# A four-layer modulated convolution on one core: stage 1 of the weight chain by six products, one sum of the inputs by an accumulating DMA, three sums an iteration sooner

## The chip, the cores and the metric

One core of a Trainium2 chip runs the whole kernel. The metric is the device time of one launch in microseconds (us). Each kernel was run several times; the median is quoted with the lowest and the highest run.

The engines carry the profile's names: PE multiplies matrices (PEld is the loading of its weights, which overlaps), DVE and POOL do elementwise work, ACT does scaled copies, SP starts most DMAs. Each takes its instructions in order and waits on semaphores for the others.

## The reference

128 sequences `x` of 64 channels and 1024 positions go through four convolutions of three taps. The weights of each are scaled per sequence and input channel by a style vector and normalised per sequence and output channel; the second doubles the length, the last halves it, both with a blur by (1, 3, 3, 1) / 8. The result is added to `x`. Cut to what matters:

```python
TYPES = ('same', 'upsample', 'same', 'downsample')

def _layer(x, style, w, b, mw, mb, typ):
    s = style @ mw.T + mb
    weight = SCALE * w * s[:, None, :, None]
    demod = lax.rsqrt(jnp.sum(weight * weight, axis=(2, 3)) + EPS)
    weight = weight * demod[:, :, None, None]
    if typ == 'same':
        out = jax.vmap(_conv_same)(x, weight) + b[None, :, None]
    elif typ == 'upsample':
        out = jax.vmap(_conv_up)(x, weight.transpose(0, 2, 1, 3)) + b[None, :, None]
        out = _blur(out, 2.0 * blur_k, (1, 1))
    elif typ == 'downsample':
        xb = _blur(x, blur_k, (2, 2))
        out = jax.vmap(_conv_down)(xb, weight) + b[None, :, None]
    return out

out = x
for i, typ in enumerate(TYPES):
    out = _layer(out, style, weights[i], biases[i], mod_w[i], mod_b[i], typ)
return x + out
```

Everything is float32. No layer has a nonlinearity, so for each sequence the four layers and the sum with `x` are one convolution of nine taps (apart from the ends, which are computed by themselves). The kernel uses that.

## The kernel before

**Units and tiles.** The 128 sequences are 32 units of four (`NQ` = 32). Two sequences share the 128 partitions (64 channels each) and two more lie side by side, so that a group of four matmuls of 64 by 64 serves the four sequences at once. A unit's input tile `X` holds three planes: the positions by their remainder modulo 3.

**The weight chain.** For each unit the four layers' weights are multiplied into nine taps. `scale3` (ACT) makes `wd`, the last layer's three taps with their scales, and beside them sums of taps (`w3x`). *Stage 1* multiplies them by the third layer's taps to the five taps `S`. Each product of one tap by one tap is a block of 64 columns. The first three units and unit 6 go through `stage1`, the plain nine blocks; the other 28 go through `stage1_a` and `stage1_b`, which share products: with a0, a1, a2 and b0, b1, b2 the taps, a0b1 + a1b0 is (a0+a1)(b0+b1) - a0b0 - a1b1. Between the halves ACT copies `psS` with a scale into `S`; after the second half DVE subtracts (line 481) and POOL adds (line 484). *Stage 2* (`stage2`, with `share`) brings in the second layer and the blur and gives `R`; ACT copies it out, POOL forms two sums of taps (`r_sums`, line 638). *Stage 3* (`stage3_b`, `stage3_a`) brings in the first layer and gives `Wf`, from which DVE combines the taps `H` (`combine_a`, `combine_b`).

**The convolution.** It goes by five products of three groups each instead of nine taps. The inputs are sums of the planes: `G` holds planes half of one minus another (`in_g01`, `in_g2`, both DVE, line 712); T1 and T2 are sum and difference of two planes of `G` (`in1`, line 776, and `in2`, line 781, both POOL, one tile `T12`); T0 and T4 lie in `T04` (`in04`, DVE, line 790); T3 is a difference of planes of `X` (`in3`, DVE, line 761). `conv0` to `conv4` are the products, all through line 803; conv4 gathers in `Y`, the others in `psA`. `sum1` and `sum2` (DVE) put partial results together, `output` (ACT) writes them with scale and bias, `store` sends them off.

**The order.** It is written out by hand. `turn_of(q)` is one turn of the main loop and works on several units at once: the end of the convolution of unit q (conv2, conv4, conv0, outputs), the beginning for n = q + 1 (conv3, conv1), stages 2 and 3 and the input sums for c = q + 2, and stage 1 for s = q + 4. Units 0 to 3 go through `early_turn`, the last three through code of their own. `T12` and `T04` have two buffers, `G` has one, `psS`, `psR` and `psW` share one pair of PSUM banks. `SIDE`, `LATE` and `TABLES` hang small jobs of DVE and POOL, mostly for the ends of the sequences, into certain turns.

**What one turn does, in order.** PE: stage 2 of c, conv2 of q, `stage3_b` of c, conv4 of q, `stage3_a` of c, conv3 of n, `stage1_a` of s, conv0 of q, `stage1_b` of s, `share` for c + 1, conv1 of n. DVE: sum2, the combining of taps, T0/T4 of n, the sums for `share` (line 501), the two parts of `G` of c with a side job and stage 1's subtraction between them, sum1, T3 of c. POOL: `r_sums`, T2 of n, the addition in `S`, T1 of c.

Of the kernel before, what the change touches and what calls it, by code (L numbers as in the profile page):

```python
# [54 lines left out]
C = 64  # L55
K = 3
# [7 lines left out]
def kernel(  # L64
# [30 lines left out]
    gpool = ctx.enter_context(tc.tile_pool(name="gpool", bufs=1))  # L95
# [308 lines left out]
    w3x = const.tile([P, 5, C], F32, name="w3x")  # L404
    w2n = const.tile([P, 5, C], F32, name="w2n")
# [9 lines left out]
    def scale3(q, engs=(nc_a, nc_a)):  # L415
# [3 lines left out]
        for j in range(2):  # L419
            t = wd_pool.tile([P, 5, C], F32, tag="wd", name=f"wd{q}_{j}")  # L420
# [23 lines left out]
    EVEN = slice(0, K, 2)  # L444

    def stage1(q, pool=None, engs=(nc_a, nc_a), between=None):
# [9 lines left out]
        for r in range(2):  # L456
            scaled_copy(engs[r], flat(st[r][:, 1:6]), ps[r][:, : 5 * C], tB[:, q, r : r + 1])
# [3 lines left out]
    def stage1_a(q, ps=None):  # L461
# [3 lines left out]
        tap_matmul(ps, wd, 2, 2, w2n[:, 0, :], EVEN, first=True)  # L465
        tap_matmul(ps, wd, 3, 2, w2n[:, 2, :], EVEN)
        tap_matmul(ps, wd, 1, 1, w2n[:, 1, :], slice(1, 2))
        st, t = s_tiles(q)
        for r in range(2):
            scaled_copy(nc_a, flat(st[r][:, :4]), ps[r][:, C : 5 * C], tBn[:, q, r : r + 1])  # L470
        chain[q] = wd, ps, st, t

    def stage1_b(q):

        wd, ps, st, t = chain[q]
        tap_matmul(ps, wd, 2, 1, w2n[:, 3, :], slice(3, 4))
        tap_matmul(ps, wd, 4, 1, w2n[:, 4, :], slice(4, 5), last=True)
        for r in range(2):
            p1 = st[r][:, 0:1, :].to_broadcast([P, 2, C])
            sums = ps[r][:, 2 * C : 6 * C].rearrange("c (a b o) -> c a b o", a=2, b=2)[:, :, 0]  # L480
            nc_v.scalar_tensor_tensor(
                st[r][:, 4:6, :], sums, tB[:, q, r : r + 1], p1, op0=ALU.mult, op1=ALU.subtract
            )
        nc_g.tensor_add(t[:, :, 2], t[:, :, 2], t[:, :, 0])  # L484
# [14 lines left out]
    def share_sums(q):  # L499
        t = whole[q]  # L500
        nc_v.tensor_add(t[:, :, 6:8], t[:, :, 1:5:3], t[:, :, 2:6:3])
# [13 lines left out]
    def share(q, ps):  # L515
# [3 lines left out]
        chain_matmul(p12, E[:, 2], chain[q], slice(6, 7))  # L519
        chain_matmul(p34, E[:, 6], chain[q], slice(6, 7))  # L520
        chain_matmul(p34, E[:, 5], chain[q], slice(7, 8), True)
# [1200 lines left out]
```

## Time and profile before

| | |
|---|---|
| median of 3 runs | 475.84 us (475.61 to 476.85) |
| span of the profiled execution | 475.5 us |
| DVE busy | 417.3 us (88%) |
| ACT busy | 312.0 us (66%) |
| POOL busy | 165.8 us (35%) |
| queue of SP's DMAs, share of 16 DMA engines | 46.3% |
| matmul records of line 803, 64x340 | 3840 |

The profiled execution is one of its own. Its span lies 0.34 us below the median of the runs; a difference worked out against the span is carried over to the median as it is. Times in the timeline count from the start of the span. A row of the timeline merges equal instructions that follow each other; its second number is the time from the start of the first to the end of the last. In a matmul's row that end lies behind the start of the next row, since a matmul's results come out after the next one has entered; how long PE is taken is therefore read from the start of one row to the start of the next.

### The profile page before, as it was taken

The page shows a single profiled execution, that of the slowest core. Times are in us where ns is not written, and L with a number is a line of the kernel's source. Part 1 is how long each engine was busy: PE and PEld are TensorE (multiplying, and loading weights), DVE is VectorE, ACT ScalarE, POOL GpSimd, SP SyncE. Part 2 cuts the span into 40 slices and gives each one's busy share as a digit, 9 for nine tenths or more (in the row PEclk, how much of TensorE's full clock was granted, in tenths as well). Part 3 has the DMA queues.
Part 4 walks back from the last instruction along what each step waited for, and adds up shares of the span by engine and source line. Part 5 has one row for each costly group of instructions (what it writes and reads, how often), then busy time and mean ns, then how long its engine had stood idle before and what let it go on. Part 6 is the DMA issues. An engine that isn't in the chain of part 4 may idle for free.

```text
span 475.5 us, 26771 instructions
## 1 busy us (share of the span) xinstructions
PE 469.7 (99%) x11932; PEld 349.5 (74%) x11932; DVE 417.3 (88%) x694; ACT 312.0 (66%) x711; POOL 165.8 (35%) x200
## 2 busy tenths in 40 slices
PE   9999999999999999999999999999999999999996
PEld 6987788777678876677776677766788787876653
DVE  3889998879989998899979899979998999999896
ACT  4565657577766676766667666667666777766464
POOL 3634033664444342233432233422333423243200
PEclk9999999999999999999999999999999999999999
DMA  5237456535445554345544454543555544455225
GB/s 176 71 115 224 150 151 180 152 113 177 139 145 166 166 166 136 123 150 169 163 150 126 130 168 152 178 124 121 152 164 169 164 145 147 148 152 161 80 91 193
DMA packets 52707, 70.71 MB, mean 149 GB/s; under 512 B 6000, under 2 KB 50672, under 8 KB 52592
## 3 DMA queue, kind: packets, MB, share of 16 engines
q1 hardware_dynamic: 52368, 68.78, 46.3%
q8 instruction: 93, 1.52, 1.4%
q10 hardware_dynamic: 224, 0.22, 0.1%
q14 instruction: 22, 0.18, 0.1%
HBM read 35.36 MB, written 33.62 MB: 145 GB/s over the span
## 4 chain that ended last, share of the span: by engine, by line
PE 99%; DVE 0%; ACT 0%; issue 0%
PE psA L803 47%; PE Y L803 12%; PE psR L506 9%; PE psW L621 7%; PE psA L621 7%; PE psS L428 6%; PE psR L589 5%; PE psA L506 2%; PE Y L1044 2%; PE Y L183 1%; PE Y L379 1%; PE psM L220 0%; PE psE L1044 0%; PE Y L255 0%; DVE o L882 0%; PE psM L255 0%
## 5 line engine op out<-in xcount | busy, mean ns | idle before, releaser
L803 PE MATMUL psA<-T,H 64*64 64x340 f32 x2304 | 185.9, 446 | 0.0
L803 PEld LDWEIGHTS psA<-T,H 64*64 64x64 f32 x2304 | 90.7, 133 | 46.9 <-issue 2.5
L712 DVE SCALAR_TENSOR_TENSOR G<-X 128x1376 f32<-128x1376 f32 (+2 forms) x65 | 78.0, 1206 | 0.2
L776 POOL TENSOR_TENSOR T<-G 128x684 f32<-128x684 f32 x28 | 46.3, 1652 | 73.7 <-DVE G L712 73.7
L484 POOL TENSOR_TENSOR S<-S 128x128 f32<-128x128 f32 x28 | 21.6, 772 | 139.7 <-ACT S L399 139.6
L399 ACT ACTIVATE R<-psR,tC 128x448 f32<-128x448 f32 x63 | 36.6, 631 | 43.6 <-PE psR L506 25.8
L803 PE MATMUL psA<-T,Wf 64*64 64x340 f32 x768 | 63.7, 446 | 0.0
L803 PE MATMUL Y<-T,Wf 64*64 64x340 f32 x768 | 62.4, 451 | 0.0
L712 DVE SCALAR_TENSOR_TENSOR Y<-m,psA 128x340 f32<-128x340 f32 x62 | 32.0, 516 | 28.2 <-PE psA L803 26.9
L399 ACT ACTIVATE psW<-psA 128x128 f32<-128x128 f32 x100 | 19.3, 268 | 49.1 <-PE psA L621 45.0
L790 DVE TENSOR_TENSOR T<-G 128x1368 f32<-128x1368 f32 (+1 forms) x33 | 50.8, 1541 | 0.0
L399 ACT ACTIVATE Wf<-psW,t 128x256 f32<-128x256 f32 (+2 forms) x76 | 32.7, 480 | 26.7 <-PE psW L621 26.4
L761 DVE TENSOR_TENSOR T<-X 128x684 f32<-128x684 f32 x32 | 47.7, 1492 | 0.0
L506 PE MATMUL psR<-S,E 64*64 64x64 f32 (+1 forms) x1472 | 46.8, 237 | 0.0
L781 POOL TENSOR_TENSOR T<-G 128x684 f32<-128x684 f32 x28 | 46.5, 1660 | 0.0
L428 PEld LDWEIGHTS psS<-wd,w2n 64*64 64x64 f32 x1120 | 35.1, 133 | 12.9 <-issue 0.3
L506 PEld LDWEIGHTS psR<-S,E 64*64 64x64 f32 x1472 | 39.5, 134 | 4.9 <-ACT psR L529 0.2
L803 PEld LDWEIGHTS Y<-T,Wf 64*64 64x64 f32 x768 | 30.3, 132 | 16.8
L803 PEld LDWEIGHTS psA<-T,Wf 64*64 64x64 f32 x768 | 29.8, 133 | 14.5
L880 ACT ACTIVATE o<-psA,tb,td 128x340 f32<-128x340 f32 x63 | 37.1, 648 | 5.0 <-PE psA L803 2.8
L880 ACT ACTIVATE o<-y,tb,td 128x340 f32<-128x340 f32 x62 | 38.5, 678 | 0.0
L880 ACT ACTIVATE o<-Y,tb,td 128x340 f32<-128x340 f32 x62 | 36.1, 639 | 2.8 <-PE Y L803 2.0
(180 smaller groups left out, 840.4 us busy)
## 6 DMA issues: line engine op xcount, KB each, us to landing
out<-o SPq DMA_DIRECT2D x191, 170.0 KB, 2.6
X<-in_x SPq DMA_DIRECT2D x150, 172.0 KB, 3.4
X<-in_x SPq DMA_DIRECT2D x14, 516.0 KB, 5.0
par<-in_params SPq DMA_DIRECT2D x3, 192.0 KB, 3.8
Xe<-in_x_ends SPq DMA_DIRECT2D x1, 512.0 KB, 4.5
out<-Oe SPq DMA_DIRECT2D x2, 96.0 KB, 2.1
out<-o ACTq DMA_DIRECT2D x1, 170.0 KB, 2.8
par<-in_params SPq DMA_DIRECT2D x1, 160.0 KB, 2.7
```

Source lines behind the costliest of these rows:

```text
L399: nc_a.activation(dst, src, AF.Copy, scale=f)
L428: nc.tensor.matmul(ps[r][cols, at * C : (at + n) * C], weight[rows], wd[c if r == 0 else 1 - c][rows, taps], start=first, stop=last, skip_ ...
L506: nc.tensor.matmul(dst[r][cols], weight[rows], st[c if r == 0 else 1 - c][rows, slots, :], start=False, stop=last, skip_group_check=True,)
L589: nc.tensor.matmul(ps[r][cols, lo * C : (lo + m) * C], E[rows, e + 2, :], src[rows, a, :], start=(n == 0), stop=(n == 8), skip_group_check ...
L621: nc.tensor.matmul(dst[r][cols], weight[rows], t[rows, c, slots, :], start=first, stop=last, skip_group_check=True,)
L712: nc_v.scalar_tensor_tensor(out, x, f, y, op0=ALU.mult, op1=op)
L761: nc_v.tensor_sub(t[:, pairs, 0, :NJ], plane(X, 3, pairs), plane(X, 1, pairs))
L776: eng.tensor_add(t[:, :, 0, :NJ], plane(g, 2), plane(g, 1))
L781: eng.tensor_sub(t[:, :, 1, :NJ], plane(g, 2), plane(g, 1))
L790: nc_v.tensor_sub(t[:, pairs, :, :NJ], both(a, PL), both(b, 1))
L803: nc.tensor.matmul(ps[s][cols, :NB], w, Ts[q, tag][rows, c, i, g : g + NB], start=(g == 0 and (m == 3 or alone)), stop=(g == K - 1), skip_ ...
L880: nc_a.activation(dst, src, AF.Identity, bias=add, scale=d3)
```

## The change

It has three parts.

**Stage 1 by six products.** `w3x` and `w2n` get a sixth block, the sum of taps 0 and 2. `stage1_a` now makes the products a0b0, a2b2, a1b1 in one block each, `stage1_b` the three products of sums. That leaves out one block of 64 columns in each of the 28 units. ACT copies the first three products by four copies of 128 columns in place of two of 256; POOL forms a0b0 + a2b2 - a1b1 by two instructions (lines 472 and 473) in place of one, and DVE's subtraction, now 192 columns wide in place of 128, reads POOL's result. The plain `stage1` takes its nine blocks as three of 192 columns. The slots of `S` are numbered anew, and what reads them follows.

**T1 by DMA.** `in1` on POOL is replaced from the sixth turn (q = 5) on by `in1_dma`: a DMA that POOL issues right behind `r_sums` and that adds one plane of `G` onto the other in place. conv1 reads T1 out of `G`. `G` gets two buffers for that; to make room, the tile `raw` moves into `Ye` and `g1` into `nw`.

**Other sums sooner.** T0/T4 of a unit are formed at the end of the turn before (behind T3), T2 on POOL likewise ahead of it, and both parts of `G` stand together, ahead of the side job and of stage 1's subtraction.

```diff
-    gpool = ctx.enter_context(tc.tile_pool(name="gpool", bufs=1))
+    gpool = ctx.enter_context(tc.tile_pool(name="gpool", bufs=2))
...
         for t, src in ((w3x, w3), (w2n, woi[2])):
-            nc_g.tensor_add(t[:, K:], src[:, : K - 1], src[:, 1:])
+            nc_g.tensor_add(t[:, K : K + 2], src[:, : K - 1], src[:, 1:])
+            nc_g.tensor_add(t[:, K + 2], src[:, 0], src[:, 2])
...
-        for k, (at, at1) in enumerate(((0, 3), (3, 1), (1, 4))):
-            tap_matmul(ps, wd, at, 2, woi[2][:, k, :], EVEN, first=k == 0)
-            tap_matmul(ps, wd, at1, 1, woi[2][:, k, :], slice(1, 2), last=k == K - 1)
+        for k in range(K):
+            tap_matmul(ps, wd, k, K, woi[2][:, k, :], slice(0, K), first=k == 0, last=k == K - 1)
...
     def stage1_a(q, ps=None):
-        tap_matmul(ps, wd, 2, 2, w2n[:, 0, :], EVEN, first=True)
-        tap_matmul(ps, wd, 3, 2, w2n[:, 2, :], EVEN)
-        tap_matmul(ps, wd, 1, 1, w2n[:, 1, :], slice(1, 2))
+        for n, (i, at) in enumerate(((0, 1), (2, 3), (1, 4))):
+            tap_matmul(ps, wd, at, 1, w2n[:, i, :], slice(i, i + 1), first=n == 0)
         st, t = s_tiles(q)
         for r in range(2):
-            scaled_copy(nc_a, flat(st[r][:, :4]), ps[r][:, C : 5 * C], tBn[:, q, r : r + 1])
+            ends = ps[r][:, C : 5 * C].rearrange("c (a b o) -> c a b o", a=2, b=2)[:, :, 0]
+            scaled_copy(nc_a, st[r][:, 0:5:4, :], ends, tBn[:, q, r : r + 1])
+        for r in range(2):
+            middle = ps[r][:, None, 4 * C : 5 * C].to_broadcast([P, 2, C])
+            scaled_copy(nc_a, st[r][:, 5:8:2, :], middle, tBn[:, q, r : r + 1])
+        nc_g.tensor_add(t[:, :, 6], t[:, :, 0], t[:, :, 4])
+        nc_g.tensor_sub(t[:, :, 6], t[:, :, 6], t[:, :, 5])
...
     def stage1_b(q):
-        tap_matmul(ps, wd, 2, 1, w2n[:, 3, :], slice(3, 4))
-        tap_matmul(ps, wd, 4, 1, w2n[:, 4, :], slice(4, 5), last=True)
+        for n, (i, at) in enumerate(((3, 1), (4, 3), (5, 2))):
+            tap_matmul(ps, wd, at, 1, w2n[:, i, :], slice(i, i + 1), last=n == K - 1)
         for r in range(2):
-            p1 = st[r][:, 0:1, :].to_broadcast([P, 2, C])
-            sums = ps[r][:, 2 * C : 6 * C].rearrange("c (a b o) -> c a b o", a=2, b=2)[:, :, 0]
             nc_v.scalar_tensor_tensor(
-                st[r][:, 4:6, :], sums, tB[:, q, r : r + 1], p1, op0=ALU.mult, op1=ALU.subtract
+                flat(st[r][:, 1:4]),
+                ps[r][:, C : 4 * C],
+                tB[:, q, r : r + 1],
+                flat(st[r][:, 5:8]),
+                op0=ALU.mult,
+                op1=ALU.subtract,
             )
-        nc_g.tensor_add(t[:, :, 2], t[:, :, 2], t[:, :, 0])
...
+    def in1_dma(q):
+        g = Gs[q]
+        nc_g.dma_start(plane(g, 2), plane(g, 1), accum_op=ALU.add)
+        first_of[q] = g[:, :, :PL]
...
     def turn_of(q):
             conv2(q)
             r_sums(c, nc_g)
+            in1_dma(n)
             sum2(q)
-            in2(n, nc_g)
...
-        in04(n)
+        if entry:
+            in04(n)
         if sharing(q):
             share_sums(c + 1)
         in_g2(c)
+        in_g01(c)
         side(SIDE, q)
...
             stage1_b(s)
-        in_g01(c)
...
+        in2(c, nc_g)
         sum1(n)
         in3(c)
         side(LATE, q)
-        if s == NQ:
-            in04(c)
-        in1(c, nc_g)
+        in04(c)
```

The rows below are those of one turn, q = 12 (so n = 13, c = 14, s = 16), first before and then after the change.

PE, stage 1 of unit 16, first half: each row is one matmul, `psS_0` and `psS_1` are the two banks, `wd_0` and `wd_1` the two tiles of scaled taps. Before, the first half:

```order
L428 MATMUL psS_0_3977<-wd_0_3798,w2n 64x128
L428 MATMUL psS_0_3977<-wd_1_3800,w2n 64x128
L428 MATMUL psS_1_3978<-wd_1_3800,w2n 64x128
L428 MATMUL psS_1_3978<-wd_0_3798,w2n 64x128
```

Twice these four and then four of 64x64 make up the first half before, 8 of 64x64 the second half: 20 matmuls. After:

```order
L429 MATMUL psS_0_4015<-wd_0_3836,w2n 64x64
L429 MATMUL psS_0_4015<-wd_1_3838,w2n 64x64
L429 MATMUL psS_1_4016<-wd_1_3838,w2n 64x64
L429 MATMUL psS_1_4016<-wd_0_3836,w2n 64x64
```

Three times these four now stand in each half, 24 matmuls, all of 64 columns.

DVE from the end of the combining of taps to sum2's first step (`Y<-`) in the next turn. Before:

```order
L790 TENSOR_TENSOR T_13_3996<-G_3729 128x4x342
L501 TENSOR_TENSOR S_3721<-S_3721 128x2x128
L712 SCALAR_TENSOR_TENSOR G_3999<-X_105 128x2x342
L1066 TENSOR_TENSOR Ye_161<-Ye_161,c_156 128x64x6
L481 SCALAR_TENSOR_TENSOR S_3991<-psS_0_3977,tB,S_3991 128x128
L481 SCALAR_TENSOR_TENSOR S_3991<-psS_1_3978,tB,S_3991 128x128
L712 SCALAR_TENSOR_TENSOR G_3999<-X_105 128x2x688
L712 SCALAR_TENSOR_TENSOR y_13_4062<-psA_3884,m_13_3994 128x680
L761 TENSOR_TENSOR T_14_4064<-X_105 128x2x342
L712 SCALAR_TENSOR_TENSOR Y<-m_13_3994,psA_3884 128x340 x2
```

After:

```order
L506 TENSOR_TENSOR S_3752<-S_3752 128x2x128
L717 SCALAR_TENSOR_TENSOR G_4039<-X_105 128x2x342
L717 SCALAR_TENSOR_TENSOR G_4039<-X_105 128x2x688
L1082 TENSOR_TENSOR Ye_159<-Ye_159,c_155 128x64x6
L482 SCALAR_TENSOR_TENSOR S_4029<-psS_0_4015,tB,S_4029 128x192
L482 SCALAR_TENSOR_TENSOR S_4029<-psS_1_4016,tB,S_4029 128x192
L717 SCALAR_TENSOR_TENSOR y_13_4107<-psA_3922,m_13_4036 128x680
L766 TENSOR_TENSOR T_14_4109<-X_105 128x2x342
L803 TENSOR_TENSOR T_14_4111<-G_4039 128x4x342
L717 SCALAR_TENSOR_TENSOR Y<-m_13_4036,psA_3922 128x340 x2
```

T0/T4 went from the head of this stretch (for unit 13) to its tail (for unit 14), right ahead of `Y<-`; the large part of `G` went ahead of the side job (`Ye`) and of stage 1's subtraction.

POOL over the same turn. Before:

```order
L638 TENSOR_TENSOR R_3858<-R_3858 128x2x128
L781 TENSOR_TENSOR T_13_3796<-G_3729 128x2x342
L484 TENSOR_TENSOR S_3991<-S_3991 128x2x64
L776 TENSOR_TENSOR T_14_4066<-G_3999 128x2x342
```

After:

```order
L643 TENSOR_TENSOR R_3896<-R_3896 128x2x128
L786 DMA G_3762<-G_3762 128x2x342
L472 TENSOR_TENSOR S_4029<-S_4029 128x2x64
L473 TENSOR_TENSOR S_4029<-S_4029 128x2x64
L794 TENSOR_TENSOR T_14_4105<-G_4039 128x2x342
```

The DMA for unit 13 stands behind `R`'s sums, where T2 of unit 13 was; T1's place at the turn's end is taken by T2 of unit 14, and stage 1 has two POOL instructions, which are ahead of the subtraction on DVE now.

More of the change, by code (lines that the diff above doesn't have):

```diff
@@ L401, in scaled_copy @@
             eng.tensor_scalar(dst, src, f, None, op0=ALU.mult)
-    w3x = const.tile([P, 5, C], F32, name="w3x")
-    w2n = const.tile([P, 5, C], F32, name="w2n")
+    w3x = const.tile([P, 6, C], F32, name="w3x")
+    w2n = const.tile([P, 6, C], F32, name="w2n")
     def split_weights():
@@ L518, in share @@
         p12, p34 = ([b[:, i:j] for b in ps] for i, j in zip(at, at[1:]))
[L519 to L521 removed]
+        chain_matmul(p12, E[:, 2], chain[q], slice(5, 6))
+        chain_matmul(p34, E[:, 6], chain[q], slice(5, 6))
+        chain_matmul(p34, E[:, 5], chain[q], slice(6, 7), True)
         shared_ps[q] = [b[:, at[0] : at[2]] for b in ps]
@@ L795, in product @@
         tag, i = SLOT[m]
+        if m == 1 and q in first_of:
+            src = first_of[q]
+        else:
+            src = Ts[q, tag][:, :, i]
         for g in groups:
@@ L805, in product @@
                         w,
-                        Ts[q, tag][rows, c, i, g : g + NB],
+                        src[rows, c, g : g + NB],
                         start=(g == 0 and (m == 3 or alone)),
@@ L1560 @@
     q, n, c = NQ - 3, NQ - 2, NQ - 1
+    in1_dma(n)
     stage2(c)
     conv2(q)
-    in2(n, nc_g)
     stage3(c, 0)
```

40 lines of the change are left out of this document (20 added, 20 removed).

## The prediction

> **What bounds the kernel now.** I read the page's first lines, then the waits of PE, then one turn of the main loop in the timeline.
>
> ```profile
> span 475.5 us, 26771 instructions
> ## 1 busy us (share of the span) xinstructions
> PE 469.7 (99%) x11932; PEld 349.5 (74%) x11932; DVE 417.3 (88%) x694; ACT 312.0 (66%) x711; POOL 165.8 (35%) x200
> ```
>
> ```profile
> PE Y L183 <- DVE eps L155: 1.0, 1, 1.0
> PE psA L621 <- issue: 0.2, 1, 0.2
> ```
>
> The two rows of the second fence are all that PE ever waited for: 1.2 us in 475.5. But a PE row counts as busy while results drain, so 99% does not show that matmuls enter without pause. That takes the starts of neighbouring rows. Turn q = 12:
>
> ```profile
> 210.53 0.73 PE L428 MATMUL psS<-wd,w2n 64*64 64x128 f32 x24
> 211.08 1.90 PE L803 MATMUL psA<-T,Wf 64*64 64x340 f32 x24
> 212.80 0.41 PE L428 MATMUL psS<-wd,w2n 64*64 64x64 f32 x16
> 213.03 0.53 PE L506 MATMUL psA<-S,E 64*64 64x64 f32 x24
> 213.38 1.90 PE L803 MATMUL psA<-T,H 64*64 64x340 f32 x24
> 215.10 0.40 PE L506 MATMUL psR<-S,E 64*64 64x128 f32 x8
> ```
>
> 24 matmuls of 340 columns take 1.72 us from start to start at both places where the rows show it (211.08 to 212.80, 213.38 to 215.10): 0.211 ns per column and record. 16 of 64 columns take 0.23 us (212.80 to 213.03): 14.4 ns each, 0.225 ns per column. So the price of a matmul is nearly its columns, and they follow each other without a gap. PE sets the time, and whatever shortens its stream shortens the span, if nobody else comes late.
>
> **The PE part.** Each matmul of the program is two records in the trace: the order has 20 rows for one unit's stage 1, the timeline 24 + 16 records. The first half takes 0.55 us (210.53 to 211.08); 8 of its records have 64 columns, 8 x 14.4 = 0.115 us, which leaves 0.435 us for 16 of 128 columns, 27.2 ns each. The second half takes 0.23 us, together 0.78 us. Afterwards it is 48 records of 64 columns: 48 x 14.4 ns = 0.69 us. Gain 0.09 us a unit, 28 units, **2.5 us**. Splitting a 128 in two costs 28.8 against 27.2 ns; that is in the sum.
>
> The four plain stage 1 units have 24 records of 128 columns and 24 of 64 and get 24 of 192. A 128 and a 64 together cost 27.2 + 14.4 = 41.6 ns, a 192 at 0.211 to 0.225 ns a column 40.5 to 43.2: between 0.1 us less and 0.2 us more for all four, which I take as nothing.
>
> **DVE, by the same turn.** What it must not miss is sum2's first step (`Y`), since conv4 adds onto `Y`.
>
> ```profile
> 210.03 1.58 DVE L790 TENSOR_TENSOR T<-G 128x1368 f32<-128x1368 f32 x1
> 211.53 0.42 DVE L501 TENSOR_TENSOR S<-S 128x256 f32<-128x256 f32 x1
> 211.86 0.87 DVE L712 SCALAR_TENSOR_TENSOR G<-X 128x684 f32<-128x684 f32 x1
> 212.64 0.81 DVE L1066 TENSOR_TENSOR Ye<-Ye,c 128x384 f32<-128x384 f32 x1
> 213.38 0.60 DVE L481 SCALAR_TENSOR_TENSOR S<-psS,tB,S 128x128 f32<-128x128 f32 x2
> 213.90 1.58 DVE L712 SCALAR_TENSOR_TENSOR G<-X 128x1376 f32<-128x1376 f32 x1
> 215.42 0.87 DVE L712 SCALAR_TENSOR_TENSOR y<-psA,m 128x680 f32<-128x680 f32 x1
> 216.21 1.81 DVE L761 TENSOR_TENSOR T<-X 128x684 f32<-128x684 f32 x1
> 219.00 1.07 DVE L712 SCALAR_TENSOR_TENSOR Y<-m,psA 128x340 f32<-128x340 f32 x2 [0.98 <-PE psA L803]
> ```
>
> ```profile
> 455.07 0.87 DVE L761 TENSOR_TENSOR T<-X 128x684 f32<-128x684 f32 x1
> ```
>
> From start to start, in the new order: sums for `share` at 210.03, `G` 0.33 later, its large part after 0.78, the side job after 1.52, stage 1's subtraction after 0.74, at 213.40, where it is today (213.38). It grows by 64 columns twice; 128x384 takes some 0.56 us in the combining of taps against 0.30 here, so 0.05 us each, 0.1 together: done about 214.1. Then `y` waits for conv1, whose results end at 213.38 + 1.90 = 215.28, less the gained 0.09: 215.2, 0.2 us sooner than now, when DVE itself was late.
>
> T3 has two durations: 1.81 us at 216.21, beside POOL's T1 (215.64, below), and 0.87 us at 455.07, with POOL idle. T1 has left POOL, and T2 takes its place earlier (below), so I take 0.87. T3 starts at 216.0, T0/T4 at 216.8 and ends at 218.4; `Y` is due at 219.00 - 0.09 = 218.9. **Reserve 0.5 us**: T0/T4 is hidden in DVE's idle 0.98 us and in what T3 gives back. Without the short T3 it would end at 219.3, 0.4 us late. In one turn a late job stands between T3 and T0/T4:
>
> ```profile
> 231.98 0.74 DVE L1016 SCALAR_TENSOR_TENSOR g<-par,g 128x192 f32<-128x192 f32 x2
> ```
>
> There 0.74 exceeds the reserve by **0.2 us**, once. The first turn of the main loop forms T0/T4 of two units. I take that as nothing, since DVE there waits 2.39 us for ACT just ahead of stage 1's subtraction, and the work before it can move into that:
>
> ```profile
> 100.74 0.14 DVE L1524 MEMSET Y<- 128x96 f32 x1 [2.39 <-ACT o L880]
> ```
>
> **ACT and POOL.**
>
> ```profile
> 206.54 0.77 ACT L399 ACTIVATE psW<-psA 128x128 f32<-128x128 f32 x4 [1.90 <-PE psA L621]
> ...
> 211.29 0.84 ACT L399 ACTIVATE S<-psS,tBn 128x256 f32<-128x256 f32 x2 [0.32 <-PE psS L428]
> ...
> 213.80 0.63 ACT L529 COPY psR<-psA 128x256 f32<-128x256 f32 x2
> ```
>
> ```profile
> 204.72 0.73 POOL L638 TENSOR_TENSOR R<-R 128x256 f32<-128x256 f32 x1 [1.27 <-ACT R L399]
> ...
> 212.21 0.82 POOL L484 TENSOR_TENSOR S<-S 128x128 f32<-128x128 f32 x1 [5.16 <-ACT S L399]
> ...
> 215.64 1.65 POOL L776 TENSOR_TENSOR T<-G 128x684 f32<-128x684 f32 x1 [2.61 <-DVE G L712]
> ```
>
> Four copies of 128 columns took 0.77 us at 206.54, two of 256 take 0.84 at 211.29: ACT loses nothing. The first half of stage 1 ends 0.2 us sooner, so the copies start at 211.1 and the first two are done about 211.5. POOL's two instructions at 0.82 each then run from 211.6 to 213.25; DVE wants the result at 213.4. If POOL is later than that, the subtraction is, and after it the copies into `psR` (213.80 to 214.43, about 0.13 later by the wider subtraction), which stage 2 needs at 215.10 - 0.09. That is another 0.45 us, so POOL may be 0.6 us late before PE feels it. T2 follows at 213.3 and ends about 214.95, 1 us ahead of T3. The wider `wd` copies (384 for 320 columns) lie in ACT's wait before `R`.
>
> **The DMA.** It is issued when `R`'s sums are done, 204.72 + 0.73 = 205.45, and conv1 wants it at 213.38 less 0.09, 213.3: a window of **7.8 us**. Behind it in POOL's queue stands the addition at 211.6, so its issue may hold POOL for 6 us. On SP's queue nothing moves. The trace has no DMA of POOL's and no accumulating one; the nearest rows (size of each, median us to landing):
>
> ```profile
> out<-o SPq DMA_DIRECT2D x191, 170.0 KB, 2.6
> X<-in_x SPq DMA_DIRECT2D x150, 172.0 KB, 3.4
> X<-in_x SPq DMA_DIRECT2D x14, 516.0 KB, 5.0
> ```
>
> It adds 128 x 684 floats, 342 KB, reading two operands and writing one. Below: 2.6 us, the quickest row. Above: 1026 KB, all three streams, at the slope of the two `X` rows (1.6 us for 344 KB) 5.0 + 2.4 = 7.4 us, and as much for making its descriptors as POOL takes for T1 itself, 1.65: 9.05 us. I take 342 KB on the same slope, 4.2 us, and half of the 1.65: 5.0 us, nearest to the `X` rows. It is hidden behind conv4, conv3 and conv0; at the upper bound it is 1.2 us late in each of 25 transfers, 30 us. [...]
>
> **Sum.** -2.5 + 0.2 = -2.3 us. The span goes from 475.5 to 473.2, the median from 475.84 to **473.5 us**. What a measurement can tell from no change is some 0.3%, 1.4 us.
>
> **The rivals.** *The DMA lands late.* It takes the place of no wait: today conv1 finds T1 long done. It decides from 7.9 us after `R`'s sums (2.3 us over 25 turns are 0.1 us beyond the window); each further 0.1 us costs 2.5 us, at the upper bound 475.8 - 2.3 + 30 = 503.5 us, at 0.25 us beyond it 479.8. For it: it shares the DMA engines with what SP sends, which already takes nearly half of them:
>
> ```profile
> q1 hardware_dynamic: 52368, 68.78, 46.3%
> ```
>
> Against it: my middle price leaves 2.8 us.
>
> *The short reserves are eaten.* POOL's instructions vary; if the subtraction or T0/T4 comes 0.1 us too late for PE in 24 turns, 2.4 us are lost, and the time stays at 475.9, within 0.3%.
>
> *PE pays by the instruction.* The grouped rows of stage 1 seem to say so:
>
> ```profile
> L428 PE MATMUL psS<-wd,w2n 64*64 64x64 f32 x672 | 21.1, 217 | 0.0
> L428 PE MATMUL psS<-wd,w2n 64*64 64x128 f32 x448 | 18.3, 269 | 0.0
> ```
>
> By these sums it is 31.4 ns a record of 64 columns and 40.8 of 128: 1344 x 31.4 ns = 42.2 us against 39.4, 2.8 us slower, 478.6 us. Against it: the busy sum counts each run's draining, and starts show 14.4 ns.
>
> [...]
>
> **How the numbers follow.** The forecast 0.76; short reserves 0.08; late DMA 0.11; price by instruction 0.03; descriptors 0.02. Faster 0.76, within 0.3% 0.08, slower 0.16. The forecast's own range is 473.1 (no late job, the plain units' tenth and another from shorter waits) to 474.3 (a third of the gain lost to small waits). For 8 in 10 it reaches down to 472.8 and over the case of short reserves up to 476.5; what is left out is mostly the late DMA.
>
> **What would show it.** A turn from conv4 to conv4 now, length and busy times:
>
> ```profile
> 206.28:220.12 13.84, 13.84 (x393) 9.79 (x385) 12.73 (x20) 9.79 (x23) 4.81 (x5) 1.00 0.45 141
> ```
>
> Right: 13.75 us, stage 1's two halves 0.35 us each; T3 at 0.87; DVE idle about 0.5 us before `Y`; PE waiting for nothing at conv1. Wrong: waits of PE on the DMA at conv1's first matmul, or on DVE at `Y`; T3 still at 1.8 us; POOL's two instructions over 1 us each with the `psR` copies behind them.

## The result, and the profile after

The change made the kernel slower: 482.55 us (median of 6 runs, 480.33 to 485.78) against 476.49 (6 runs, 475.61 to 477.17), ratio 1.0134 with a 95% interval of 1.0113 to 1.0154. The profiled execution took 482.7 us with a span of 480.9, 5.4 more than the span of before. In each of its six runs the time is 1.8 us above the span, and in the runs of before that the experiments took along 1.8 is the rule as well, so the profiled execution of before (475.5) was probably one of about 477.3.

The first lines of the page after, its lines of POOL's DMA queue and of the queue of the kind "instruction", which I take to load PE's instructions (used further down), and the row of the new DMA (size, median us to landing):

```profile
span 480.9 us, 27143 instructions
...
PE 471.9 (98%) x12060; PEld 348.0 (72%) x12060; DVE 409.3 (85%) x694; ACT 324.5 (67%) x767; POOL 182.1 (38%) x230
...
q0 software_dynamic: 6800, 8.76, 11.0%
q8 instruction: 94, 1.54, 1.5%
...
G<-G POOLq DMA_DIRECT2D x25, 342.0 KB, 6.1
```

DVE has 8 us less to do than before; ACT has 12.5 more and POOL 16. The waits of PE, all there are (us, times, longest):

```profile
PE psR L511 <- ACT psR L534: 1.4, 1, 1.4
PE Y L183 <- DVE eps L155: 1.0, 1, 1.0
PE psR L511 <- issue: 0.5, 1, 0.5
PE psA L820 <- DVE y L717: 0.4, 1, 0.4
PE Y L820 <- issue: 0.2, 1, 0.2
```

None is on the DMA. Only the second of them was there before. Two of the new ones lie ahead of stage 2 (L511): one on ACT's copies into `psR`, one on nothing that the profile shows. The 0.4 us on sum1's `y` lie at 87.0, in the turn q = 3. The turn q = 12 after, rows of POOL, DVE and ACT from the first half of stage 1 on, with the first row of stage 2:

```profile
211.69 2.36 DVE L717 SCALAR_TENSOR_TENSOR G<-X 128x684 f32<-128x684 f32 x2
...
212.43 1.14 ACT L399 ACTIVATE S<-psS,tBn 128x128 f32<-128x128 f32 x4
...
213.15 1.22 POOL L472 TENSOR_TENSOR S<-S 128x128 f32<-128x128 f32 x1 [5.23 <-ACT S L399]
...
214.45 0.65 POOL L473 TENSOR_TENSOR S<-S 128x128 f32<-128x128 f32 x1
...
215.06 1.65 POOL L794 TENSOR_TENSOR T<-G 128x684 f32<-128x684 f32 x1
...
215.14 0.74 DVE L482 SCALAR_TENSOR_TENSOR S<-psS,tB,S 128x192 f32<-128x192 f32 x2 [0.35 <-POOL S L473]
215.64 0.63 ACT L534 COPY psR<-psA 128x256 f32<-128x256 f32 x2 [0.33 <-DVE S L482]
...
216.35 0.41 PE L511 MATMUL psR<-S,E 64*64 64x128 f32 x8
...
217.46 0.86 DVE L766 TENSOR_TENSOR T<-X 128x684 f32<-128x684 f32 x1
...
218.24 1.58 DVE L803 TENSOR_TENSOR T<-G 128x1368 f32<-128x1368 f32 x1
...
220.25 1.07 DVE L717 SCALAR_TENSOR_TENSOR Y<-m,psA 128x340 f32<-128x340 f32 x2 [0.44 <-PE psA L820]
```

Much of it is as forecast: T3 takes 0.86, T0/T4 are done in time, DVE is idle 0.44 us ahead of `Y`. But the subtraction waits for POOL, whose first addition runs beside the large part of `G` and takes 1.22 us, and the four ACT copies take 1.14. The `psR` copies end at 216.27, 0.08 us ahead of stage 2: in this turn PE does not wait yet. Three turns in the view of windows (start and end, length, busy times; the first of the main loop, q = 12, and a late one), with the first one before in the second fence:

```profile
91.62:108.14 16.52, 16.44 (x396) 12.12 (x388) 13.71 (x23) 10.77 (x25) 13.05 (x19) 1.00 0.54 131
193.86:207.62 13.76, 13.76 (x401) 9.83 (x393) 12.03 (x20) 10.28 (x25) 5.35 (x6) 1.00 0.66 174
397.67:411.55 13.88, 13.88 (x397) 10.46 (x392) 12.16 (x20) 10.27 (x25) 5.48 (x6) 1.00 0.69 187
```

```profile
91.08:106.97 15.89, 15.89 (x388) 12.38 (x380) 12.39 (x22) 10.37 (x23) 11.44 (x17) 1.00 0.45 137
```

An undisturbed turn gains the 0.08 us (13.84 to 13.76). The first turn of the main loop loses 0.63, late turns give the gain back.

**The table for all that follows.** The first conv4 matmul of a turn cuts each trace in pieces: from turn 0 to q = 5 ("early"), from there to q = 28 ("main"). "Border" adds up PE's stalls of over 60 ns at what I take for the borders of its instruction blocks, explained in its place below. Times are medians, ratios against runs of before on the same chip.

| kernel | us | ratio (95%) | early | main | border |
|---|---|---|---|---|---|
| before | 476.49 | 1 | 75.81 | 327.42 | 0.77 |
| after | 482.55 | 1.0134 (1.0113 to 1.0154) | 76.80 | 331.04 | 1.72 |
| six products only | 477.54 | 1.0029 (1.0010 to 1.0049) | 76.64 | 327.24 | 0.66 |
| order only | 478.51 | 1.0060 (1.0041 to 1.0079) | 75.48 | 329.07 | 0.00 |
| order and DMA | 479.87 | 1.0075 (1.0049 to 1.0102) | 76.40 | 331.31 | 1.76 |
| six products and order | 480.86 | 1.0096 (1.0064 to 1.0129) | 76.80 | 330.03 | 0.70 |
| the same, borders shifted | 481.02 | 1.0095 (1.0076 to 1.0114) | 76.92 | 330.66 | 0.59 |
| after, borders shifted | 483.13 | 1.0155 (1.0130 to 1.0179) | 77.16 | 331.67 | 2.79 |
| before, unread DMAs | 476.21 | 1.0000 (0.9986 to 1.0014) | 75.74 | 327.17 | 0.56 |

The span's 5.4 us are 0.2 ahead of turn 0, 1.0 early, 3.6 main and the rest from q = 28 on. The early 75.81 of before holds 0.4 us in turn q = 2 that most traces of the same program do not have; the kernel with one small DMA (below), the same program there, took 75.36.

### The profile page after: what moved, and what is told of

It reads as the page before. It is cut to its first block, busy times and chain, and to the rows that moved or that the text cites. A ratio compares the mean times of both kernels' runs of the same rounds, so it can differ in the third digit from the quotient of the medians.

```text
span 480.9 us, 27143 instructions
## 1 busy us (share of the span) xinstructions
PE 471.9 (98%) x12060; PEld 348.0 (72%) x12060; DVE 409.3 (85%) x694; ACT 324.5 (67%) x767; POOL 182.1 (38%) x230
## 3 DMA queue, kind: packets, MB, share of 16 engines
q0 software_dynamic: 6800, 8.76, 11.0%
## 4 chain that ended last, share of the span: by engine, by line
PE 95%; DVE 3%; issue 1%; ACT 0%; DVEq 0%; ACTq 0%
PE psA L820 45%; PE Y L820 11%; PE psR L511 10%; PE psA L626 7%; PE psW L626 7%; PE psS L429 5%; PE psR L594 4%; PE psA L511 2%; PE Y L1060 2%; PE Y L183 1%; DVE H L717 1%; PE Y L379 1%; DVE Ue L1118 0%; DVE G L717 0%; PE psM L220 0%
## 5 line engine op out<-in xcount | busy, mean ns | idle before, releaser
L820 PE MATMUL psA<-T,H 64*64 64x340 f32 x1704 | 140.2, 446 | 0.4 <-DVE y L717 0.4
L820 PEld LDWEIGHTS psA<-T,H 64*64 64x64 f32 x1704 | 71.8, 133 | 31.7 <-issue 2.6
L472 POOL TENSOR_TENSOR S<-S 128x128 f32<-128x128 f32 x28 | 29.6, 1056 | 143.2 <-ACT S L399 143.2
L511 PE MATMUL psR<-S,E 64*64 64x64 f32 (+1 forms) x1472 | 49.8, 239 | 1.5 <-ACT psR L534 1.4
L643 POOL TENSOR_TENSOR R<-R 128x256 f32<-128x256 f32 x24 | 18.1, 752 | 87.4 <-DVE T L803 45.9
L794 POOL TENSOR_TENSOR T<-G 128x684 f32<-128x684 f32 x28 | 46.8, 1671 | 6.1 <-PE psA L820 6.0
L511 PEld LDWEIGHTS psR<-S,E 64*64 64x64 f32 x1472 | 43.6, 134 | 7.5 <-ACT psR L534 4.3
L820 PE MATMUL psA<-G,H 64*64 64x340 f32 x600 | 47.7, 446 | 0.0
L717 DVE SCALAR_TENSOR_TENSOR y<-psA,m 128x680 f32<-128x680 f32 x31 | 26.8, 865 | 19.7 <-PE psA L820 16.1
L429 PEld LDWEIGHTS psS<-wd,w2n 64*64 64x64 f32 x1344 | 32.6, 134 | 13.0 <-issue 0.3
```

Source lines behind the costliest of these rows:

```text
L429: nc.tensor.matmul(ps[r][cols, at * C : (at + n) * C], weight[rows], wd[c if r == 0 else 1 - c][rows, taps], start=first, stop=last, skip_ ...
L472: nc_g.tensor_add(t[:, :, 6], t[:, :, 0], t[:, :, 4])
L511: nc.tensor.matmul(dst[r][cols], weight[rows], st[c if r == 0 else 1 - c][rows, slots, :], start=False, stop=last, skip_group_check=True,)
L643: eng.tensor_add(t[:, :, 7:9], t[:, :, 2:6:3], t[:, :, 3:7:3])
L717: nc_v.scalar_tensor_tensor(out, x, f, y, op0=ALU.mult, op1=op)
L794: eng.tensor_sub(t[:, :, 1, :NJ], plane(g, 2), plane(g, 1))
```

## The experiments: the three parts, one by one

**Six products only.** Of the diff stage 1, the places of `S` and the moves of `raw` and `g1` remain; order, T1 and one buffer of `G` are as before.

> Stage 1 by six products alone; T1 stays on POOL, G has one buffer and all sums stand where they stood before. Three causes are weighed for the changed kernel's loss. C (chain): POOL's two instructions and DVE's subtraction behind the moved part of G come too late for the copies into psR, and stage 2 waits. F (fetch): PE runs out of instructions at the borders of the 16 KB blocks of its stream, since blocks of 64-column matmuls are used up faster and the DMA of POOL's slows the blocks' loading. O (outside): a kernel with a DMA of POOL's spends some 1.5 us more outside of its span. C, if POOL's two instructions are the fault wherever G stands: 476 to 478 us, waits of DVE on POOL S. C, if it is the moved part of G: about 474.5. F: the stream is as dense, but no DMA slows its loading: 474 to 475.5. O: time less span as in the kernel before, under 0.5 us.

**Order and DMA only.** The rest of the diff, with stage 1 of before.

> Stage 1 by seven products as before, with the accumulating DMA, two buffers of G and the new order of the sums. C: no POOL result stands ahead of the subtraction, only the moved part of G: at most 1 us of waits, 476.5 to 477.5 plus what O takes. F: blocks load as slowly as in the changed kernel while PE needs its instructions as fast as before: 1 to 2 us of stalls at block borders. O: 1.5 us between time and span. O and F together: 478 to 480 us.

**All but the DMA.** The changed kernel with POOL's addition at the DMA's place.

```
-            in1_dma(n)
+            in1(n, nc_g)
```

> The changed kernel with T1 formed by POOL at the place where it issues the DMA; everything else as changed. C: waits at psR and at Y stay as they are, some 2.5 us: 477 to 479 us. F: stalls without a semaphore at block borders fall from about 2 us to the kernel before's 0.5 to 0.8. O: the 1.5 us outside of the span go. F and O right, C small: 475 to 477 us; all three: about 478.

**One small DMA.** Before, with one DMA of POOL's near the end that nobody waits for (`nc_g.dma_start(spare, idn)`).

> The kernel before with one DMA of 32 KB issued by POOL near the end, which nothing waits for. O: the time rises by about 1.5 us, to 478 us, and the span stays at about 475.5. If the time outside comes from many or large DMAs and not from having one, the time stays within 0.3 us of the kernel before. C and F expect nothing here.

**Order only.** The same edit as "all but the DMA", on "order and DMA only".

> Seven products as before; the new order of the sums and two buffers of G, but T1 by POOL's own addition at the place of the DMA. Chain theory (the moved sums run beside POOL's additions, stage 1's subtraction and the psR copies come late, stage 2 waits): the order alone loses most of what order and DMA together lost (3.6 us), some 2.2 us, so 478.4 us (477.8 to 479.3), with PE waiting for the psR copies in the turns q = 13 and q = 18, near 230 and 305 us. Rival, all of that loss is the DMA's: 476.2 us and no wait on psR.

The small DMA did nothing (476.12, ratio 1.0007, 0.9991 to 1.0022), so what lies outside the span is no matter of the change. Each of the three parts loses by itself or with another: six products 1.3 us, the order 2.7; both together 4.6, which the intervals do not tell from their sum of 4.0; the DMA on top of both 1.7. Six products lose early, 0.8 us against this trace of before and 1.3 against the 75.36, and only come out even in the main part, where 23 units should gain 2.0. Of the early loss 0.34 us are PE's wait for `y` in the turn q = 3, which this trace has as the changed kernel's does. Order alone loses nothing early and 1.6 us in the main part, where PE waits at two places. The row of these waits, and turn q = 13:

```profile
PE psR L506 <- ACT psR L529: 1.5, 2, 1.0
...
226.49 2.35 DVE L1027 SCALAR_TENSOR_TENSOR nw<-par,nw 128x192 f32<-128x192 f32 x2
...
226.85 1.78 POOL L789 TENSOR_TENSOR T<-G 128x684 f32<-128x684 f32 x1
...
228.76 0.60 DVE L481 SCALAR_TENSOR_TENSOR S<-psS,tB,S 128x128 f32<-128x128 f32 x2
...
229.60 0.60 PE L506 MATMUL psR<-S,E 64*64 64x128 f32 x6 [0.48 <-ACT psR L529]
```

POOL's T2 has moved beside DVE's side job, which takes 2.35 us in place of 1.00 before (first row below); the subtraction, the `psR` copies and stage 2 are late. The changed kernel has the same in turn q = 18. Before, in q = 13 (one row) and in q = 18, and then after, in q = 18:

```profile
226.48 1.00 DVE L1016 SCALAR_TENSOR_TENSOR g<-par,g 128x192 f32<-128x192 f32 x2
...
299.06 1.39 DVE L1102 SCALAR_TENSOR_TENSOR Ue<-b1s,Ue 64x64 f32<-64x64 f32 x4
...
300.48 0.61 DVE L481 SCALAR_TENSOR_TENSOR S<-psS,tB,S 128x128 f32<-128x128 f32 x2
```

```profile
301.36 3.00 DVE L1118 SCALAR_TENSOR_TENSOR Ue<-b1s,Ue 64x64 f32<-64x64 f32 x4
...
302.26 1.69 POOL L794 TENSOR_TENSOR T<-G 128x684 f32<-128x684 f32 x1
...
304.39 0.74 DVE L482 SCALAR_TENSOR_TENSOR S<-psS,tB,S 128x192 f32<-128x192 f32 x2
...
304.90 0.63 ACT L534 COPY psR<-psA 128x256 f32<-128x256 f32 x2 [2.19 <-DVE S L482]
...
305.31 0.60 PE L511 MATMUL psR<-S,E 64*64 64x128 f32 x6 [1.38 <-ACT psR L534]
```

## The experiments: the chain to stage 2

**Large part of `G` behind the subtraction again.**

```
         in_g2(c)
-        in_g01(c)
         side(SIDE, q)
...
             stage1_b(s)
+        in_g01(c)
```

> The changed kernel with one line put back: the large part of G stands behind stage 1's subtraction again. Chain theory: POOL's first addition falls from 1.22 to about 0.5 us, DVE's waits for POOL before the subtraction (7.6 us) nearly vanish, PE's idle time before stage 2 that ends with the psR copies falls from 5.7 us to under 1.5, and the time falls by 3 to 4 us to 479 (478 to 480). Rival one, T2 then runs beside T3 again, T3 takes 1.8 us, T0/T4 end late and conv4 waits for Y 0.3 to 0.4 us a turn: not below 482 us. Rival two, the loss is the DMA's through the instruction blocks: unchanged at 482.5 us.

487.13 us, ratio 1.0232 (1.0210 to 1.0254). Rival one came, with more than its price. Turn q = 11:

```profile
199.71 0.44 POOL L472 TENSOR_TENSOR S<-S 128x128 f32<-128x128 f32 x1 [5.24 <-ACT S L399]
...
200.27 0.46 POOL L473 TENSOR_TENSOR S<-S 128x128 f32<-128x128 f32 x1
...
201.14 0.74 DVE L482 SCALAR_TENSOR_TENSOR S<-psS,tB,S 128x192 f32<-128x192 f32 x2 [1.56 <-PE psS L429]
...
203.52 1.67 POOL L794 TENSOR_TENSOR T<-G 128x684 f32<-128x684 f32 x1 [2.79 <-DVE G L717]
...
204.07 1.86 DVE L766 TENSOR_TENSOR T<-X 128x684 f32<-128x684 f32 x1
...
205.85 1.57 DVE L803 TENSOR_TENSOR T<-G 128x1368 f32<-128x1368 f32 x1
...
206.38 1.63 POOL L643 TENSOR_TENSOR R<-R 128x256 f32<-128x256 f32 x1 [1.18 <-ACT R L399]
```

POOL's additions fall to 0.44 and 0.46, and no wait of PE on `psR` is left; that half of the theory holds. But T2 now runs beside T3 (1.86), T0/T4 run beside `R`'s sums (1.63 for 0.73), stage 3 and conv4 wait, and turns take 14.25. The overlap has only changed its victim.

**Side jobs behind the subtraction.** In the changed kernel:

```
         in_g01(c)
-        side(SIDE, q)
...
             stage1_b(s)
+        side(SIDE, q)
```

The side jobs of q = 5 and 6 then read sums that are cleared already: this kernel leaves out constants of a part of the sequences.

> The changed kernel with the side jobs of DVE moved behind stage 1's subtraction. Chain theory (a side job beside POOL's T2 takes up to twice its time and holds the subtraction, the psR copies and stage 2): PE's wait of 1.5 us for psR in turn q = 18 goes, the other turns keep their small ones, since POOL's two additions hold the subtraction there; 480.6 us (479.9 to 481.5) where the changed kernel has 482.5. Rival, the side job then holds y, T3, T0/T4 and at last Y: PE waits at conv4 in its place, not below 482.3 us.

The wait in q = 18 is gone (that turn is 1.5 us shorter, by the traces), but the time is not: 482.91 us, ratio 1.0150 (1.0116 to 1.0183). Its trace has 4.0 us of border stalls, more than any other. So it shows what held stage 2 in that turn, and not what the cure is worth.

**Copies split.** Before, with ACT's two copies of 256 columns made four of 128.

```
-            scaled_copy(nc_a, flat(st[r][:, :4]), ps[r][:, C : 5 * C], ...)
+            scaled_copy(nc_a, flat(st[r][:, :2]), ps[r][:, C : 3 * C], ...)
+        for r in range(2):
+            scaled_copy(nc_a, flat(st[r][:, 2:4]), ps[r][:, 3 * C : 5 * C], ...)
```

> The kernel before, with ACT's two copies of 256 columns between the halves of stage 1 split into four of 128. They should take 1.14 us in place of 0.84, as in the changed kernel. If ACT is part of what the early turns lose: 0.3 to 0.6 us slower, 476.7 us. Rival one, ACT has room everywhere: 476.2. Rival two, it is all of the early loss: 477.5 us.

477.08 us, ratio 1.0017 (1.0001 to 1.0033). The group of the copies, and the first turn of the main loop:

```profile
L399 ACT ACTIVATE S<-psS,tBn 128x128 f32<-128x128 f32 x112 | 32.0, 369 | 11.4 <-PE psS L428 11.4
...
90.87:107.11 16.24, 16.05 (x388) 13.02 (x379) 12.55 (x22) 10.67 (x25) 11.42 (x17) 1.00 0.51 140
```

That turn takes 16.24 us for 15.89, the early piece 75.88 where the small-DMA kernel, the same program there, took 75.36. So the copies are some 0.5 of the 1.3 us that six products lose early; the rest was not separated further.

**Six products from unit 9 on.** Six products, old order, but `stage1_a` and `stage1_b` keep seven for units 3, 4, 5, 7 and 8.

```
+    SEVEN = (3, 4, 5, 7, 8)
...
     def stage1_a(q, ps=None):
...
+        if q in SEVEN:
+            return seven_a(q, ps)
```

> Six products, old order, T1 on POOL, as in the first experiment, but units 3, 4, 5, 7 and 8, whose stage 1 lies in the early turns and the first turn of the main loop, keep seven products. If the early turns are where six products cost more than they save (1.3 us up to the sixth turn in that trace), the turns up to the sixth take what they did before, and the time is 476.3 us (475.7 to 476.9) where the first experiment had 477.5. Rival, the loss belongs to what stays (copies of 384 columns for wd, plain stage 1 in three products of 192, the new slots): 477.5 us.

**Late jobs apart.** The same, and

```
+        14: lambda: setup1(1),
...
-        18: lambda: (rest1_edges(0), rest1_edges(1)),
+        18: lambda: rest1_edges(0),
+        19: lambda: rest1_edges(1),
...
-    LATE = {13: lambda: setup1(1)}
+    LATE = {}
```

> The kernel of the experiment before it, with the second job of turn q = 13 in q = 14 and the second of q = 18 in q = 19, which had none. Chain theory: the waits at conv4 after q = 13 and at stage 2 after q = 18 (0.4 and 0.2 us in the first experiment's trace) go, 475.6 us (475.0 to 476.3), a little faster than both. Rival, they only move to the next turns: same as the experiment before it.

The early loss is gone in both (75.40 and 75.36): it belongs to six products in those turns. The first came out at 477.16 us (1.0025, 1.0008 to 1.0042) and not at 476.3, since in its trace PE waits in turn q = 13, behind the two jobs that the second takes apart:

```profile
PE Y L851 <- DVE Y L748: 1.9, 1, 1.9
```

The second took 476.05 us, ratio 0.9991 (0.9973 to 1.0008): not told apart from before. Part of the loss only moved: the turns q = 14 and q = 19, which got the jobs, take 0.6 and 0.4 us more than before. It is the best version of six products found, and no gain.

## The experiments: instruction blocks and the DMA

PE stops at places where it waits for nobody. The longest, in stage 2 of turn q = 21 after (timeline of PE; the last entry is idle time ahead of the row):

```profile
351.62 0.44 PE L511 MATMUL psR<-S,wsq 64*64 64x64 f32 x14
352.56 0.13 PEld L511 LDWEIGHTS psR<-S,wsq 64*64 64x64 f32 x1 [0.64 <-issue]
352.56 0.27 PE L511 MATMUL psR<-S,wsq 64*64 64x64 f32 x1 [0.51 <-issue]
```

The page counts 94 packets of 16 KB on a queue of the kind "instruction" (q8), and PE has 24120 matmuls and weight loads: one packet for 24120 / 94 = 256.6 of them. I numbered PE's instructions, its waits on semaphores counted with the matmuls and weight loads, in each of nine traces (before, after, the five kernels of the first section, the first shift of the borders and the first try with unread DMAs, both below). Of 29 stops over 90 ns with no wait, 26 lie at number 192 to 194 modulo 256, each 1.3 to 1.6 us after a packet of that queue had landed. So I take them for borders of instruction blocks, at which PE stops when the next block lands late; the shifts below put that to the test. By estimate a block of 64-column matmuls (128 records, each with its weight load) is used up in 128 x 14.4 ns = 1.8 us, a block of 340-column ones, at the 1.72 us that 24 records took, in 9.2 us.

**Borders shifted, before.**

```
     def stage1(q, pool=None, engs=(nc_a, nc_a), between=None):
...
+        for _ in range(8 if q == 2 else 0):
+            for r, rows in enumerate(HALF):
+                for cols in HALF:
+                    nc.tensor.matmul(ps[r][cols, :8], woi[2][rows, 0, :], wd[0][rows, 0, :8], start=True, ...)
```

> The kernel before, with 32 matmuls of 8 columns (128 PE instructions, half a block of 256) put ahead of the third unit's stage 1, whose results are overwritten. Fetch theory: all later block borders fall half a block earlier in the program, so the stalls at the instructions that stalled before (stage 3's last matmuls, turns q = 8, 22 and 25 among others) go and others appear 128 instructions away from them; the time is within 1 us of before plus the 0.2 to 0.5 us of the added matmuls. Rival, the stalls belong to those instructions: they stay where they are in the program.

The old places no longer stall; the clearest stall at a new border (0.20 us, at 403.4) lies in stage 2. The time is 478.62 us, ratio 1.0062 (1.0039 to 1.0084), more than expected; the profiled execution is the fastest of the five, with 0.7 us lost at 105.9 in a place that is no border. What the other runs lost is open.

**Borders shifted, after, with and without the DMA.** The same 32 matmuls in the changed kernel and in the one with T1 on POOL.

> The changed kernel with 32 matmuls of 8 columns (128 PE instructions) ahead of the third unit's stage 1, so that every later block of 256 instructions begins half a block earlier in the program. Block theory: the stalls at 160, 165, 348 and 353 us go, others come at the new borders, and the time moves by up to 2 us either way from 482.5. Rival, the position of the borders is of no account: 482.5 to 483.0 us, the added matmuls' own time.

> The same shift with T1 on POOL at the DMA's place. Block theory with the DMA as what delays the blocks: 1 to 2 us faster than the experiment before it, as it was without the shift (480.9 against 482.5 us), with less than 1 us of stalls at borders. Rival, the DMA is innocent and the difference was chance: the two within 0.5 us.

The stalls moved (to 162, 218, 360 and 436 us, among others), and the DMA's price came again: 483.13 against 481.02, with 2.79 against 0.59 us at borders. Once PE also waited for the DMA itself:

```profile
PE psA L831 <- DMA G<-G: 0.4, 1, 0.4
```

**DMAs that nobody reads.** Before, with one accumulating DMA a turn on a scratch tile (`nc_g.dma_start(spare[:, 0:2], spare[:, 2:4], accum_op=ALU.add)` behind `in2`). A first try had its scratch cleared by DVE ahead of turn 0:

> The kernel before, with 24 accumulating DMAs of POOL's, one a turn, 342 KB each, that add one scratch plane to another; nothing waits for them or reads them, and POOL issues each behind T2. Fetch theory (the DMA makes the blocks of PE's instructions land later): PE's stalls that no semaphore explains grow from some 0.8 us to about 1.7, and the time rises by 1.0 us to 477.2 (476.7 to 477.9). Rival, a DMA that nobody waits for costs nothing: 476.2 us, stalls as before.

477.91 us, ratio 1.0044 (1.0025 to 1.0062), but its early and main pieces are as in before; the clearing, 1.20 us on DVE, made PE wait 1.0 us at conv4 of turn 0. So it was made again with POOL clearing the scratch later (the second expectation calls this one e15), and then with the shape of the changed kernel's DMA:

> The kernel before with 24 unread accumulating DMAs, one a turn, as in the earlier experiment, but the scratch planes are cleared by POOL in the second early turn and no longer by DVE ahead of the first, where that cost 1.2 us. If such DMAs cost PE by late instruction blocks alone: 477.0 to 477.8 us. Rival, the earlier 477.9 was the clearing on DVE and the DMAs cost nothing where nobody waits: 476.2 to 476.7 us.

> As e15, POOL issues each unread DMA behind T2, but the DMA has the changed kernel's shape, two rows of 342 floats in each partition and so twice as many packets. If the packets delay PE's instruction blocks in any program: 477.2 to 478.2 us with 1 to 2 us of stalls at borders. Rival, traffic of this shape costs the kernel before nothing, and the price belongs to the changed program's own stream or to the wait for the DMA: 476.0 to 476.6 us.

476.21 and 476.07 us, ratios 1.0000 (0.9986 to 1.0014) and 0.9990 (0.9973 to 1.0008): the traffic and its packets cost this program nothing. The same DMA right behind `R`'s sums, in before and in the six-product kernel:

> The kernel before with 24 unread accumulating DMAs that now have the changed kernel's shape (rows of 342 floats, so twice as many packets) and place (right behind R's sums). If the packets or the place delay PE's blocks of instructions: 477.2 to 478.2 us with 1 to 2 us of stalls at borders. Rival, an unread DMA costs this program nothing in any shape: 476.2 to 476.6 us.

> The first experiment's kernel (six products, old order, T1 on POOL: 477.5 us) with the same unread DMAs. If the DMA's cost needs the six products' stream of 64-column matmuls, whose blocks are used up sooner: 478.5 to 479.5 us with over 1.5 us of stalls at borders, while the experiment before it stays near 476.5. Rival one, the cost needs somebody who waits for the DMA: 477.5. Rival two, it is the packets alone: both are 1 to 2 us slower.

500.76 and 505.27 us, ratios 1.0522 and 1.0607, for a reason that none of the theories held. Turn q = 11 of the first, and below it the first step of `H` before, in q = 12:

```profile
195.84 1.19 POOL L1495 DMA_DIRECT2D spare<-spare  x1
...
196.62 2.09 POOL L781 TENSOR_TENSOR T<-G 128x684 f32<-128x684 f32 x1
...
197.35 1.78 DVE L712 SCALAR_TENSOR_TENSOR H<-Wf 128x384 f32<-128x384 f32 x1
...
200.27 1.95 PE L803 MATMUL psA<-T,H 64*64 64x340 f32 x24 [0.83 <-DVE H L712]
```

```profile
206.91 0.57 DVE L712 SCALAR_TENSOR_TENSOR H<-Wf 128x384 f32<-128x384 f32 x1
```

Issuing the DMA holds POOL 1.19 us. T2 behind it now meets the combining of taps, whose first step takes 1.78 us for 0.57, and conv3 waits 0.8 us in nearly every turn. As a test of the DMA they are spoilt; as one of overlap they are the clearest.

## Why the prediction was wrong, by its own steps

- **The PE part** was right where nothing disturbs: 0.35 and 0.34 us a unit and 13.76 us a turn. "PE pays by the instruction" fell as it was priced: 64 columns still cost 14.4 ns. But 16 more PE instructions a unit move the borders, which the forecast had not seen.
- **"ACT loses nothing" failed.** I took the price of four copies from a row that writes `psW` (0.77 us); four that write `S` take 1.14, against 0.84 for two. Of the step "the first turn ... I take as nothing", 0.63 us is what came, and the copies alone give 0.35 of it. All steps were read in turn q = 12; the turns 0 to 4, where six products lose 0.8 to 1.3 us, were never looked at.
- **"POOL's two instructions at 0.82 each" failed**, and with it the reserve of 0.6 us. They take 1.22 and 0.65, since the edit itself puts the large part of `G` beside the first and the side job beside the second. The subtraction is at 215.14 in place of 213.40 + 1.34 (the shift between the traces) = 214.74, 0.4 us late. In this turn the reserve just holds (0.08 us are left); where DVE's job beside them is longer it does not. That the first takes over 1 us, with the `psR` copies behind it, is half of one sign of being wrong that the prediction named (it had both over 1 us).
- **"One late job +0.2" named the wrong job.** The jobs that cost are those ahead of the subtraction once T2 moved beside them: 1.5 us in q = 18. The prediction had T2 "1 us ahead of T3" and asked no further what else it is beside. The second rival, short reserves eaten, had the right mechanism, placed too weakly: 0.1 us in 24 turns. These waits in views after: how long stage 2 sat idle behind the `psR` copies (1.4 us of its matmuls, once, and 4.3 of its weight loads, which need not all hold PE), and what DVE waited for:

```profile
  ACT psR L534: 5.7, 11
```

```profile
DVE S L482 <- POOL S L473: 7.6, 19, 0.9
```

- **How badly work overlaps.** What rows of DVE and POOL take alone and beside each other: T3 0.86 us alone and 1.86 beside T2, a step of `H` 0.57 and 1.78, POOL's sums of `R` 0.73 and 1.63, its addition in `S` 0.44 and 1.22. In these four pairs the one that starts later ends a little less than its own time alone after the first has ended: POOL's addition ends 0.32 us after the large part of `G` (214.05), T3 0.74 after T2 (205.19), the sums of `R` 0.59 after T0/T4 (207.42), the step of `H` 0.42 after T2 (198.71). The subtraction, one of whose inputs lies in PSUM, takes 0.74 beside T2 (215.14) and 0.74 with POOL idle (201.14). What causes this was not shown. Before, such overlaps fell on T3 (1.81) and on POOL's addition (0.82), where there was room. The prediction showed both rows; it took 0.82 for the addition's own price, and used 1.81 and 0.87 for T3 alone.
- **DVE, T3, T0/T4, `Y`** came as forecast (0.86, 0.44 us idle); DVE was not what PE waits for.
- **The DMA's 5.0 us** took a median of 6.1 (4.3 to 8.5), the median inside the window of 7.8 and all inside the bounds. PE never waited for it in this trace, so the late DMA fell. No run shows the descriptors that half of the 1.65 us and the chance of 0.02 stand for, nor the three streams of the upper bound: the trace after shows POOL held by the issue for 1.19 us on the median and 1.37 at most (25 times line 786) while DVE works, and the page 342 KB an issue, 8.76 MB in all. It does cost 1.7 and 2.1 us in the pairs with six products, with 1.0 and 2.2 more of border stalls. The third pair, order and DMA against order only, has 1.8 more of border stalls, but its ratios (1.0075 and 1.0060) are not told apart. Why the stalls come with the new order and not with unread DMAs in the old program stays open: there packets, shape and traffic cost nothing; the wait for the DMA was not tried by itself, and the two kernels with the place of its issue were spoilt.
- **The offset of 0.34 us** between span and time is 1.8, so the profiled execution that the sum started from took some 0.8 us more than the median. The forecast gain of 2.3 us stays as it is, from 476.5 to 474.2; only the absolute 473.5 was set too low.

In sum, by the lengths of the turns: the 2.0 us of gain in the main part are there where a turn is undisturbed, and against them stand 1.0 us early, about 1.7 in turn q = 18, 1 of additional border stalls, and what is left, some 3 us, in pieces of 0.1 to 0.6 us spread over the turns. That these are waits ahead of stage 2 and conv4 is likely by the views above and was not separated further.

## What to carry to other kernels

An order fixes which rows of POOL and DVE meet, and a step's price may hold only for its present neighbour, as here T3's (0.86 us alone, 1.86 beside T2), not the subtraction's (0.74 both ways): after a move, list for every row what now runs beside it, and price it by a row with the same neighbour, or let the later of the two begin where the earlier ends. Read the stages at the ends of the program apart from the steady turn, and price an instruction by one with the same destination (four copies of 128 columns took 0.77 us into `psW`, 1.14 into `S`). A PE stream can stop where it waits for nobody: here for 0.00 to 2.79 us in the traces of the table, at what I take for the borders of its own instruction blocks.

## What the runs showed of the hardware

In the changed kernel's trace 94 packets of 16 KB land on the queue of the kind "instruction", one for 256.6 of PE's matmuls and weight loads; a packet takes 1.2 us on the mean (up to 2.9). In nine traces 26 of 29 stops of PE of over 90 ns without a wait lie at number 192 to 194 modulo 256, and PE goes on 1.3 to 1.6 us after a packet has landed. From this I conclude that PE takes its instructions in blocks of 256 and stops when one lands late; the view of waits names no cause for such a stop. An accumulating DMA of 342 KB from SBUF to SBUF holds POOL for 1.19 us and lands 6.1 us after its issue in the changed kernel (medians of 25). Read by nobody, in the kernel before the change, it took 4.7 us when issued behind T2, 4.8 there with the changed kernel's rows of 342 floats, and 7.0 with the same rows right behind `R`'s sums: in these three runs the time went with the place of its issue, not with the length of its rows.
